# Node stage of a graph layer in pieces inside the edge loop, instead of a stage of its own behind it

## The chip, the cores and the metric

The kernel runs on one core of a Trainium2 chip. Its engines are TensorE (PE; PEld is its weight load), VectorE (DVE), ScalarE (ACT), GpSimd (POOL, "Pool" in the text) and SyncE (SP, which only issues DMAs here). Each engine works through its own list of instructions in order and waits on semaphores of the others. The metric is the device time of one execution in microseconds (us): 4080.77 before the change, the median of three runs (4079.7 to 4087.65).

## What is computed

A graph layer with attention over incoming edges, then a residual and a layer norm. There are 12,500 nodes with 64 features and 400,000 edges with 64 features, sorted by destination; the destinations are denser at low node numbers (12500 u² for uniform u).

```python
h_src = x[src]; h_dst = x[dst]
e = leaky_relu(concat([h_src, h_dst, edge]) @ W_attn + b_attn, 0.01)
m = concat([h_src, edge]) @ W_ne
ex = exp(e - segment_max(e, dst)[dst])
alpha = ex / segment_sum(ex, dst)[dst]
z = segment_sum(alpha[:, None] * m, dst)
out = relu(concat([x, z]) @ W_out)
return layernorm(x + out)
```

The kernel uses that W_ne is linear: it adds up alpha times (edge features, source features), 128 numbers for each node, and multiplies the sums by W_ne and the lower half of W_out at the end, as one 128x64 matrix named both.

## The kernel before

The sorted path (sorted_path, from line 40) makes a table of x with one more column, the source's part of the score, in DRAM, and windows of the destinations' parts. Then it goes over the edges. A group is 512 edges, four for each of the 128 partitions; there are 782 groups. A part is up to four groups (SG), and a batch is up to 24 groups, in six parts: batches 0 to 31 have 24 groups, batch 32 has 10 and batch 33 has 4 (the list sizes).

For each part, gather (line 137) loads the edge features ze by one DMA on SP's queue (L143), and the rows of the sources zx by 16 indirect DMAs on Pool (L152), one for each group and each of its four edges per partition. ze and zx have ten buffers each (ZB). scores (line 158) computes the scores of the part on DVE (L167 to L186) with one matmul on PE that spreads the windows (L163); its row wrow comes by a DMA on SP. hot marks each edge's place among the 48 nodes from its group's first destination on.

For each batch, softmax (line 226) runs segmented scans over the batch's scores. It is a serial chain of DVE, PE and ACT, from the transpose er at L254, over Exp on ACT (L298, L288), to alpha (L309, L310). Then aggregate (line 322) makes weights w from hot and alpha on DVE (L325), multiplies them with ze and zx on PE (L333, into one of four PSUM buffers named pg) and adds the result of each group on DVE to 48 columns of acc (L343). acc lies in SBUF and has a row for each of the 128 summed features and a column for each node.

The indices of batch k+2 are prepared in batch k: prepare, with a cast srcs on DVE (L121) into one of three buffers.

The node stage is in two places. In batches from 2 on, behind each part's aggregate, own_part (line 433) takes four node blocks of 128 nodes: it loads x (xb, L442, on ACT's queue), transposes it on PE (L447), copies it on ACT (L448), multiplies it with the upper half of W_out (L451), copies it (L453) and stores it in DRAM under the name early (L454). Behind the loop, finish_sorted (line 492) computes the flag that selects the general path, and both (L515 to L521), and then goes over the 98 blocks, eight at a time: it loads x again (L530) and early (L533), multiplies acc with both (L539), adds, takes relu and the residual, and normalizes (L548 to L562: eight steps on DVE, the square and the Sqrt on ACT), and stores the result (L565, L569).

The order of instructions on each engine is set when the program is built, by a scheduler that moves them by its own estimates; what a helper writes in one place can lie among the instructions of another on the engine. general_path is a second way to compute everything, which runs only where the flag is set.

Of the kernel before, what the change touches and what calls it, by code (L numbers as in the profile page):

```python
# [21 lines left out]
EPS = 1e-5  # L22
# [3 lines left out]
S = 48  # L26
BG = 32
SG = 4
# [3 lines left out]
ZB = 10  # L32
HB = 8
NBC = 4

BF16 = mybir.dt.bfloat16
EngineType = mybir.EngineType
# [2 lines left out]
def sorted_path(ctx, tc, x, dst, idx, edge, w_ne, w_attn, b_attn, w_out, out, flag):  # L40
# [38 lines left out]
    acc = const.tile([P, N + S], F32, name="acc")  # L79

    table = dram.tile([NB * P, EW], F32, name="table")
    early = dram.tile([NB * P, D], F32, name="early")
    sdflat = dram.tile([NB * P + S], F32, name="sdflat")
    shifted = dram.tile([NB * P, S], F32, name="shifted")
    wins = dram.tile([NG, S], F32, name="wins")
    d0i = const.tile([1, NG], I32, name="d0i")
    d0b = const.tile([P, NG], F32, name="d0b")
    worst = const.tile([P, 2], F32, name="worst")

    loop = ExitStack()  # L90
    chunks = loop.enter_context(tc.tile_pool(name="chunks", bufs=2))
# [254 lines left out]
    sizes = []  # L346
# [83 lines left out]
    nc.vector.memset(worst, 0.0)  # L430
    nc.vector.memset(acc, 0.0)

    def own_part(c0):

        n = min(NBC, NB - c0)
        xb = work.tile([P, NBC, D], F32, name="xb", bufs=1)
        if c0 + n > NFULL:
            nc.vector.memset(xb[:, n - 1, :], 0.0)
            nc.scalar.dma_start(out=xb[0:TAIL, n - 1, :], in_=x[NFULL * P:N, :])
        nf = min(n, NFULL - c0)  # L440
# [12 lines left out]
        nc.scalar.activation(xo[:, 0:n, :], po[:, 0:n, :], AF.Copy)  # L453
        nc.scalar.dma_start(out=early[c0 * P:(c0 + n) * P, :].rearrange("(b p) f -> p b f", p=P),  # L454
                            in_=xo[:, 0:n, :])

    def prepare(k):
        srcs, pp = prepared.pop(k) if k in prepared else indices(starts[k], sizes[k])
# [1 line left out]

    with loop:
        carry = None
        own = 0
        ready = {k: prepare(k) for k in range(2)}
        for k, G in enumerate(sizes):
            b0 = starts[k]
# [25 lines left out]
def finish_sorted(tc, x, out, acc, early, wne, wout, ident, worst, flag):  # L492

    nc = tc.nc
    N, D = x.shape
    NB = (N + P - 1) // P
    NFULL = N // P
    TAIL = N - NFULL * P
    NBF = 8
    with tc.tile_pool(name="fin", bufs=3) as fin, \  # L500
            tc.tile_pool(name="finp", bufs=2, space=bass.MemoryType.PSUM) as finp:

        bad = fin.tile([P, 2], F32, name="bad", bufs=1)
        nc.vector.tensor_scalar(bad[:, 0:1], worst[:, 0:1], float(S - 1), None, op0=OP.is_gt)
        nc.vector.tensor_scalar(bad[:, 1:2], worst[:, 1:2], 0.0, None, op0=OP.is_gt)
        pbad = finp.tile([1, 2, P], F32, name="pbad", bufs=1)
        for k in range(2):
            nc.tensor.matmul(pbad[:, k, :], bad[:, k:k + 1], ident, start=True, stop=True)
        some = fin.tile([1, 1], F32, name="some", bufs=1)
        nc.vector.tensor_reduce(some, pbad, axis=AX.XY, op=OP.max)  # L510
        nc.vector.tensor_copy(flag, some)


        pwt = finp.tile([D, P], F32, name="pwt", bufs=1)
        nc.tensor.transpose(pwt, wne, ident)  # L515
        wt = fin.tile([D, P], F32, name="wt", bufs=1)
        nc.vector.tensor_copy(wt, pwt)
        pv = finp.tile([P, D], F32, name="pwt", bufs=1)
        nc.tensor.matmul(pv, wt, wout[:, 1, :], start=True, stop=True)
        both = fin.tile([P, D], F32, name="both", bufs=1)  # L520
        nc.vector.tensor_copy(both, pv)  # L521
        for c0 in range(0, NB, NBF):
            n = min(NBF, NB - c0)
            xb = fin.tile([P, NBF, D], F32, name="xb")
            nf = min(n, NFULL - c0)
            if n > nf:
                nc.vector.memset(xb[:, n - 1, :], 0.0)
                nc.scalar.dma_start(out=xb[0:TAIL, n - 1, :], in_=x[NFULL * P:N, :])
            if nf:
                nc.scalar.dma_start(out=xb[:, 0:nf, :],  # L530
                                    in_=x[c0 * P:(c0 + nf) * P, :].rearrange("(b p) f -> p b f", p=P))
            xo = fin.tile([P, NBF, D], F32, name="xo")
            nc.sync.dma_start(out=xo[:, 0:n, :],  # L533
                              in_=early[c0 * P:(c0 + n) * P, :].rearrange("(b p) f -> p b f", p=P))
            po = finp.tile([P, NBF, D], F32, name="po")
            for j in range(n):
                k0 = (c0 + j) * P
                m = min(P, N + S - k0)
                nc.tensor.matmul(po[0:m, j, :], acc[:, k0:k0 + m], both, start=True, stop=True)  # L539
            yv = fin.tile([P, NBF, D], F32, name="yv")  # L540
            m = min(P, N + S - (c0 + n - 1) * P)
            if m < P:
                nc.vector.memset(yv[:, n - 1, :], 0.0)
                nc.vector.tensor_tensor(yv[0:m, n - 1, :], po[0:m, n - 1, :], xo[0:m, n - 1, :], op=OP.add)
                if n > 1:
                    nc.vector.tensor_tensor(yv[:, :n - 1, :], po[:, :n - 1, :], xo[:, :n - 1, :], op=OP.add)
            else:
                nc.vector.tensor_tensor(yv[:, :n, :], po[:, :n, :], xo[:, :n, :], op=OP.add)  # L548
            nc.vector.scalar_tensor_tensor(yv[:, :n, :], yv[:, :n, :], 0.0, xb[:, :n, :],
                                           op0=OP.max, op1=OP.add)  # L550
            stat = fin.tile([P, 2, NBF], F32, name="stat")
            nc.vector.tensor_reduce(stat[:, 0, :n], yv[:, :n, :], axis=AX.X, op=OP.add)
            nc.vector.tensor_scalar(stat[:, 0, :n], stat[:, 0, :n], 1.0 / D, None, op0=OP.mult)
            nc.vector.tensor_tensor(yv[:, :n, :], yv[:, :n, :],
                                    stat[:, 0, :n].unsqueeze(2).to_broadcast([P, n, D]), op=OP.subtract)
            sq = fin.tile([P, NBF, D], F32, name="sq")
            nc.scalar.activation(sq[:, :n, :], yv[:, :n, :], AF.Square)
            nc.vector.tensor_reduce(stat[:, 1, :n], sq[:, :n, :], axis=AX.X, op=OP.add)
            nc.vector.tensor_scalar(stat[:, 1, :n], stat[:, 1, :n], 1.0 / D, EPS, op0=OP.mult, op1=OP.add)
            nc.scalar.activation(stat[:, 1, :n], stat[:, 1, :n], AF.Sqrt)  # L560
            nc.vector.reciprocal(stat[:, 1, :n], stat[:, 1, :n])
            nc.vector.tensor_tensor(yv[:, :n, :], yv[:, :n, :],  # L562
                                    stat[:, 1, :n].unsqueeze(2).to_broadcast([P, n, D]), op=OP.mult)
            if nf:
                nc.sync.dma_start(  # L565
                    out=out[c0 * P:(c0 + nf) * P, :].rearrange("(b p) f -> p b f", p=P),
                    in_=yv[:, 0:nf, :])
            if n > nf:
                nc.sync.dma_start(out=out[NFULL * P:N, :], in_=yv[0:TAIL, n - 1, :])  # L569


def general_path(ctx, tc, x, dst, idx, edge, w_ne, w_attn, b_attn, w_out, out):
# [434 lines left out]
```

## Time and profile before

| | |
|---|---|
| median of three runs | 4080.77 us |
| the profiled execution | 4080.57 us |
| its span, first to last instruction | 4078.8 us |
| mean granted TensorE clock | 0.588 |
| busy: POOL, DVE, PE, PEld, ACT | 2967.8, 1875.2, 985.2, 766.8, 131.6 us |
| last row gather issued by Pool | 3970.51 us from the start |
| last add to acc | 4007.26 us, three adds, 0.68 us |
| first matmul of the stage behind the loop | 4010.83 us |
| last store issued | 4071.27 us |

A line of a timeline has the start in us, the duration in us, the engine, the line of the kernel, the operation, what it writes and reads with shapes, the count of instructions merged in the line, and in brackets how long the engine was idle before and what ended that. In a line of a group, the busy time and the mean ns of one stand behind the first bar, and the idle time before them behind the second. In a line of waits stand the total, the number and the longest. An engine named with a q (SPq, ACTq) is the queue that issues DMAs.

### The profile page before, as it was taken

What the parts mean: (1) busy time and instruction counts of PE and PEld (TensorE: products, weight loads), DVE (VectorE), ACT (ScalarE), POOL (GpSimd) and SP (SyncE); (2) the same over time, 40 slices, a digit from 0 to 9 for tenths busy, and PEclk for the clock granted to TensorE, in tenths of its full rate; (3) what the DMA queues carried; (4) which work ended last, traced back from release to release, by engine and by line L of the source; (5) the groups of instructions that cost most, each with busy time, mean ns of one, the idle gap of its engine ahead of it and who ended that gap; (6) DMA issues with size and microseconds to landing.
All of it is one profiled execution on the core that took longest, in us unless ns stands there. A gap on an engine that the chain in (4) does not pass through costs nothing.

```text
span 4078.8 us, 40728 instructions
## 1 busy us (share of the span) xinstructions
PE 985.2 (24%) x14494; PEld 766.8 (19%) x14494; DVE 1875.2 (46%) x4448; ACT 131.6 (3%) x287; POOL 2967.8 (73%) x3142
## 2 busy tenths in 40 slices
PE   0022332132222112222212222211222221122235
PEld 0022322122212011111101111211111120111225
DVE  4174443343555443455444355544335544434656
ACT  0000000000000000000000000000000000000001
POOL 6757777777777777777777777777777777777770
PEclk9985665565555555555555555555555555555555
DMA  8122332232222122222212222212222221222214
GB/s 169 29 51 60 75 75 57 46 74 60 60 60 60 28 59 59 59 60 60 48 39 59 59 60 59 60 34 54 59 60 60 60 59 27 59 58 58 55 26 96
DMA packets 315275, 239.80 MB, mean 59 GB/s; under 512 B 160574, under 2 KB 264233, under 8 KB 315062
## 3 DMA queue, kind: packets, MB, share of 16 engines
q0 software_dynamic: 100320, 104.42, 15.6%
q1 hardware_dynamic: 147462, 116.22, 9.6%
q10 hardware_dynamic: 67280, 16.45, 2.0%
q8 instruction: 117, 1.92, 0.2%
q14 instruction: 96, 0.79, 0.1%
HBM read 226.99 MB, written 12.28 MB: 59 GB/s over the span
## 4 chain that ended last, share of the span: by engine, by line
POOL 41%; DVE 22%; issue 17%; PE 11%; DMA 7%; ACT 1%; DVEq 0%; POOLq 0%; ACTq 0%
POOL zx L152 41%; DMA zx<-table,srcs 7%; PE pg L333 5%; DVE prod L167 3%; DVE y L169 3%; DVE prod L181 3%; PE fixed L163 2%; DVE hot L176 2%; PE sm L200 2%; PE sm L192 2%; DVE acc L343 1%; DVE sdst L184 1%; DVE by_row L197 1%; DVE b L273 1%; DVE w L325 1%
## 5 line engine op out<-in xcount | busy, mean ns | idle before, releaser
L152 POOL DMA_INDIRECT zx<-table,srcs x3032 | 2866.8, 946 | 956.7 <-issue 869.6
L163 PE MATMUL fixed<-wrow,ones_row 1*128 1x192 f32 x392 | 179.0, 553 | 2391.3 <-DVE prod L181 2314.5
L121 DVE CAST srcs<-pp 128x96 int32<-128x96 f32 (+2 forms) x34 | 8.6, 253 | 1587.0 <-DMA zx<-table,srcs 1521.5
L163 PEld LDWEIGHTS fixed<-wrow,ones_row 1*128 1x128 f32 x392 | 88.8, 280 | 2464.9 <-DVE prod L181 2385.1
L333 PE MATMUL pg<-w,ze 128*64 128x48 f32 x6256 | 459.3, 244 | 84.3 <-DVE w L325 73.4
L333 PEld LDWEIGHTS pg<-w,ze 128*64 128x64 f32 x6256 | 449.7, 161 | 104.5 <-DVE w L325 90.1
L333 PE MATMUL pg<-w,zx 128*64 128x48 f32 x6256 | 459.5, 244 | 5.3 <-issue 5.0
L333 PEld LDWEIGHTS pg<-w,zx 128*64 128x64 f32 x6256 | 449.7, 161 | 6.0 <-issue 6.0
L167 DVE TENSOR_TENSOR prod<-ze,fixed 128x1024 f32<-128x1024 f32 x196 | 237.6, 1212 | 86.4 <-DMA wins<-wk 49.9
L169 DVE TENSOR_REDUCE y<-prod 128x16 f32<-128x1024 f32 x196 | 237.2, 1210 | 0.0
L343 DVE TENSOR_TENSOR acc<-acc,pg 128x48 f32 x782 | 158.6, 203 | 164.1 <-PE pg L333 112.9
L325 DVE TENSOR_TENSOR w<-hot,fixed 128x768 f32<-128x768 bf16 x196 | 176.8, 944 | 42.9 <-PE pg L333 37.7
L184 DVE TENSOR_REDUCE sdst<-prod 128x16 f32<-128x768 f32 x196 | 186.1, 950 | 5.1
L181 DVE TENSOR_TENSOR prod<-hot,fixed 128x768 f32<-128x768 bf16 x196 | 185.5, 947 | 0.9
L176 DVE TENSOR_TENSOR hot<-fixed,drel 128x768 bf16<-128x768 f32 x196 | 185.9, 948 | 0.0
L115 ACT ACTIVATE nat<-raw 24x1024 f32<-24x1024 int32 (+2 forms) x34 | 35.9, 1056 | 2876.9 <-PE pp L118 2848.2
L152 POOL DMA_INDIRECT zx<-in_x_dram,srcs x96 | 93.5, 974 | 44.2 <-issue 28.7
L200 PE MATMUL sm<-ones_row,by_row 1*128 1x1 f32 x272 | 79.0, 357 | 108.9 <-DVE by_row L197 75.2
L200 PEld LDWEIGHTS sm<-ones_row,by_row 1*128 1x128 f32 x272 | 67.5, 307 | 176.8 <-DVE by_row L197 138.0
L192 PE MATMUL sm<-order,s 128*1 128x128 f32 x136 | 39.8, 396 | 194.6 <-DVE s L258 112.0
L118 PE MATMUL pp<-ident,nat 24*128 24x24 f32 (+2 forms) x272 | 36.3, 279 | 144.2 <-DVE drel L127 111.4
L174 DVE TENSOR_TENSOR y<-y,zx 128x16 f32<-128x16 f32 x196 | 37.0, 189 | 67.5 <-DMA zx<-table,srcs 64.4
(133 smaller groups left out, 1109.2 us busy)
## 6 DMA issues: line engine op xcount, KB each, us to landing
ze<-in_edge_dram SPq DMA_DIRECT2D x194, 512.0 KB
zx<-table,srcs POOLq DMA_INDIRECT x3032
table<-xt ACTq DMA_DIRECT2D x14, 227.5 KB
wrow<-wins SPq DMA_DIRECT2D x195, 0.8 KB
raw<-in_idx_dram SPq DMA_DIRECT2D x32, 96.0 KB
xb<-in_x_dram ACTq DMA_DIRECT2D x24, 128.0 KB
early<-xo ACTq DMA_DIRECT2D x24, 128.0 KB
xb<-in_x_dram ACTq DMA_DIRECT2D x12, 256.0 KB
```

Source lines behind the costliest of these rows:

```text
L152: nc.gpsimd.indirect_dma_start(out=zx[:, g, t, 0:D] if plain else zx[:, g, t, :], out_offset=None, in_=x[:, :] if plain else table[:, :], ...
L163: nc.tensor.matmul(win[:, 0:n, :], ones_row, wrow[:, 0:n, :], start=True, stop=True)
L167: nc.vector.tensor_tensor(prod[:, 0:n], ze[:, 0:n], w_edge.unsqueeze(1).to_broadcast([P, n, T, D]), op=OP.mult)
L169: nc.vector.tensor_reduce(yb, prod[:, 0:n], axis=AX.X, op=OP.add)
L176: nc.vector.tensor_tensor(hot[:, 0:n], slots.unsqueeze(1).unsqueeze(1).to_broadcast([P, n, T, S]), drel[:, :, b:b + n].rearrange("p t g -> ...
L181: nc.vector.tensor_tensor(at[:, 0:n], hot[:, 0:n], win[:, 0:n].unsqueeze(2).to_broadcast([P, n, T, S]), op=OP.mult)
L184: nc.vector.tensor_reduce(sdst[:, 0:n], at[:, 0:n], axis=AX.X, op=OP.add)
L192: nc.tensor.matmul(p[0:1, :], col, order, start=True, stop=True)
L200: nc.tensor.matmul(p[:, 0:1], by_row, ones_row[:, 0:1], start=True, stop=True)
L325: nc.vector.tensor_tensor(w[:, 0:n], hot[:, 0:n], alpha[:, :, b:b + n].rearrange("p t g -> p g t").unsqueeze(3).to_broadcast([P, n, T, S]) ...
L333: nc.tensor.matmul(pg[at:at + D, g, :], z[:, g, t, 0:D], w[:, g, t, :], start=(t == 0), stop=(t == T - 1))
L343: nc.vector.tensor_tensor(ag, ag, pg[:, g, :], op=OP.add)
```

## The change

The stage behind the loop and the early product go. In their place a function finish takes four node blocks through the whole node stage: the load of x, the transposes, both products, added up in one PSUM tile, and then relu, residual and norm, in that tile, and the store from SP's queue. A plan made when the program is built (due) says after which batch each piece can be done. It takes the square root of the share of nodes as the share of edges, with eight standard deviations (LATE) and a quarter of a group on top, and finds the first batch that starts beyond that. A piece is issued behind a part of scores in the batch that follows.

The boundaries are checked on the chip: after each batch with due pieces, one DVE operation takes the first destination of the next batch less the end of the pieces, and keeps the minimum in a column early; where it is negative, the flag is set and the general path runs. Before, early was the DRAM buffer; that buffer, its stores and loads are gone.

For this input's 34 batches the plan has 25 pieces. Pieces that start at blocks 0 to 80 (21 of them) run in batches 7 to 31, some batches with none and two with two; pieces 84 and 88 run in batch 32, 92 in batch 33, and the last, with blocks 96 and 97, behind the loop.

```diff
+LATE = 8.0
-    early = dram.tile([NB * P, D], F32, name="early")
+    early = const.tile([P, 1], F32, name="early")
+    both = const.tile([P, D], F32, name="both")
...
+    pwt = psum.tile([P, SG, P], F32, name="pg", bufs=4)
+    nc.tensor.transpose(pwt[0:D, 0, :], wne, ident)
+    wt = work.tile([D, NBC, P], F32, name="xtt", bufs=1)
+    nc.vector.tensor_copy(wt[:, 0, :], pwt[0:D, 0, :])
+    nc.tensor.matmul(pwt[:, 1, 0:D], wt[:, 0, :], wout[:, 1, :], start=True, stop=True)
+    nc.vector.tensor_copy(both, pwt[:, 1, 0:D])
...
-    def own_part(c0):
+    def finish(c0):
         n = min(NBC, NB - c0)
         xb = work.tile([P, NBC, D], F32, name="xb", bufs=1)
...
         for j in range(n):
             nc.tensor.transpose(pxt[0:D, j, :], xb[:, j, :], ident)
         nc.scalar.activation(xtt[:, 0:n, :], pxt[0:D, 0:n, :], AF.Copy)
-        po = psum.tile([P, NBC, P], F32, name="pg", bufs=4)[:, :, 0:D]
+        po = psum.tile([P, NBC, P], F32, name="pg", bufs=4)[:, 0:n, 0:D]
         for j in range(n):
-            nc.tensor.matmul(po[:, j, :], xtt[:, j, :], wout[:, 0, :], start=True, stop=True)
-        xo = work.tile([P, NBC, D], F32, name="xo", bufs=1)
-        nc.scalar.activation(xo[:, 0:n, :], po[:, 0:n, :], AF.Copy)
-        nc.scalar.dma_start(out=early[...], in_=xo[:, 0:n, :])
+            nc.tensor.matmul(po[:, j, :], xtt[:, j, :], wout[:, 0, :], start=True, stop=False)
+            nc.tensor.matmul(po[:, j, :], acc[:, (c0 + j) * P:(c0 + j + 1) * P], both, start=False, stop=True)
+        nc.vector.scalar_tensor_tensor(po, po, 0.0, xb[:, 0:n, :], op0=OP.max, op1=OP.add)
+        mean = tiny.tile([P, NBC], F32, name="mean")[:, 0:n]
+        nc.vector.tensor_reduce(mean, po, axis=AX.X, op=OP.add)
+        nc.vector.tensor_scalar(mean, mean, 1.0 / D, None, op0=OP.mult)
+        nc.vector.tensor_tensor(po, po, mean.unsqueeze(2).to_broadcast([P, n, D]), op=OP.subtract)
+        sq = work.tile([P, NBC, D], F32, name="sq", bufs=1)
+        nc.scalar.activation(sq[:, 0:n, :], po, AF.Square)
+        var = tiny.tile([P, NBC], F32, name="var")[:, 0:n]
+        nc.vector.tensor_reduce(var, sq[:, 0:n, :], axis=AX.X, op=OP.add)
+        nc.vector.tensor_scalar(var, var, 1.0 / D, EPS, op0=OP.mult, op1=OP.add)
+        nc.scalar.activation(var, var, AF.Sqrt)
+        nc.vector.reciprocal(var, var)
+        yo = work.tile([P, NBC, D], F32, name="yo", bufs=1)
+        nc.vector.tensor_tensor(yo[:, 0:n, :], po, var.unsqueeze(2).to_broadcast([P, n, D]), op=OP.mult)
+        nc.sync.dma_start(out=out[...], in_=yo[...])
...
+    due = [[] for _ in sizes]
+    k = 0
+    for c0 in range(0, NB, NBC):
+        share = min(1.0, (c0 + NBC) * P / N) ** 0.5
+        need = E * share + LATE * (E * share * (1.0 - share)) ** 0.5 + GE / 4
+        while k + 1 < len(sizes) and starts[k + 1] * GE < need:
+            k += 1
+        due[k].append(c0)
...
                 parts.append((g0, n, ze, zx, hot))
+                if done:
+                    finish(done.pop(0))
...
                 aggregate(g0, n, ze, zx, hot, b0, fac if g0 == b0 else None)
-                if own < NB and k > 1:
-                    own_part(own)
-                    own += NBC
-        while own < NB:
-            own_part(own)
-            own += NBC
-    finish_sorted(tc, x, out, acc, early, wne, wout, ident, worst, flag)
+            done += due[k]
+            if due[k] and k + 1 < len(sizes):
+                nc.vector.scalar_tensor_tensor(early, d0b[:, starts[k + 1]:starts[k + 1] + 1],
+                                               -float((due[k][-1] + NBC) * P), early, op0=OP.add, op1=OP.min)
+        bad = tiny.tile([P, 3], F32, name="bad")
...
+        nc.vector.tensor_scalar(bad[:, 2:3], early, 0.0, None, op0=OP.is_lt)
...
+        nc.vector.tensor_reduce(some, pbad, axis=AX.XY, op=OP.max)
+        nc.vector.tensor_copy(flag, some)
+        for c0 in done:
+            finish(c0)
```

More of the change, by code (lines that the diff above doesn't have):

```diff
@@ L431, in sorted_path @@
     nc.vector.memset(acc, 0.0)
-    def own_part(c0):
+    pwt = psum.tile([P, SG, P], F32, name="pg", bufs=4)
[5 more added lines that the diff above has]
+    def finish(c0):
         n = min(NBC, NB - c0)
         xb = work.tile([P, NBC, D], F32, name="xb", bufs=1)
-        if c0 + n > NFULL:
+        nf = min(n, NFULL - c0)
+        if n > nf:
             nc.vector.memset(xb[:, n - 1, :], 0.0)
             nc.scalar.dma_start(out=xb[0:TAIL, n - 1, :], in_=x[NFULL * P:N, :])
-        nf = min(n, NFULL - c0)
         if nf:
@@ L448, in own_part @@
         nc.scalar.activation(xtt[:, 0:n, :], pxt[0:D, 0:n, :], AF.Copy)
-        po = psum.tile([P, NBC, P], F32, name="pg", bufs=4)[:, :, 0:D]
+        po = psum.tile([P, NBC, P], F32, name="pg", bufs=4)[:, 0:n, 0:D]
         for j in range(n):
-            nc.tensor.matmul(po[:, j, :], xtt[:, j, :], wout[:, 0, :], start=True, stop=True)
-        xo = work.tile([P, NBC, D], F32, name="xo", bufs=1)
-        nc.scalar.activation(xo[:, 0:n, :], po[:, 0:n, :], AF.Copy)
-        nc.scalar.dma_start(out=early[c0 * P:(c0 + n) * P, :].rearrange("(b p) f -> p b f", p=P),
-                            in_=xo[:, 0:n, :])
+            nc.tensor.matmul(po[:, j, :], xtt[:, j, :], wout[:, 0, :], start=True, stop=False)
+            nc.tensor.matmul(po[:, j, :], acc[:, (c0 + j) * P:(c0 + j + 1) * P], both, start=False, stop=True)
@@ new lines, in finish @@
+        var = tiny.tile([P, NBC], F32, name="var")[:, 0:n]
[5 more added lines that the diff above has]
+        nc.vector.tensor_tensor(yo[:, 0:n, :], po, var.unsqueeze(2).to_broadcast([P, n, D]), op=OP.mult)
+        if nf:
+            nc.sync.dma_start(out=out[c0 * P:(c0 + nf) * P, :].rearrange("(b p) f -> p b f", p=P),
+                              in_=yo[:, 0:nf, :])
@@ L457, in prepare @@
+        if n > nf:
+            nc.sync.dma_start(out=out[NFULL * P:N, :], in_=yo[0:TAIL, n - 1, :])
+    due = [[] for _ in sizes]
[6 more added lines that the diff above has]
+        due[k].append(c0)
+    nc.vector.memset(early, 0.0)
     def prepare(k):
@@ L462, in sorted_path @@
         carry = None
-        own = 0
+        done = []
         ready = {k: prepare(k) for k in range(2)}
@@ L482, in sorted_path @@
                 aggregate(g0, n, ze, zx, hot, b0, fac if g0 == b0 else None)
-                if own < NB and k > 1:
-                    own_part(own)
-                    own += NBC
-        while own < NB:
-            own_part(own)
-            own += NBC
-    finish_sorted(tc, x, out, acc, early, wne, wout, ident, worst, flag)
[L492 to L503, printed above, removed]
+            done += due[k]
@@ L504, in finish_sorted @@
+            if due[k] and k + 1 < len(sizes):
+                nc.vector.scalar_tensor_tensor(early, d0b[:, starts[k + 1]:starts[k + 1] + 1],
+                                               -float((due[k][-1] + NBC) * P), early, op0=OP.add, op1=OP.min)
+        bad = tiny.tile([P, 3], F32, name="bad")
         nc.vector.tensor_scalar(bad[:, 0:1], worst[:, 0:1], float(S - 1), None, op0=OP.is_gt)
         nc.vector.tensor_scalar(bad[:, 1:2], worst[:, 1:2], 0.0, None, op0=OP.is_gt)
-        pbad = finp.tile([1, 2, P], F32, name="pbad", bufs=1)
@@ L507, in finish_sorted @@
-        for k in range(2):
+        nc.vector.tensor_scalar(bad[:, 2:3], early, 0.0, None, op0=OP.is_lt)
+        pbad = psum.tile([P, 3, P], F32, name="sm")[0:1]
+        for k in range(3):
             nc.tensor.matmul(pbad[:, k, :], bad[:, k:k + 1], ident, start=True, stop=True)
-        some = fin.tile([1, 1], F32, name="some", bufs=1)
+        some = tiny.tile([1, 1], F32, name="some")
         nc.vector.tensor_reduce(some, pbad, axis=AX.XY, op=OP.max)
         nc.vector.tensor_copy(flag, some)
-        pwt = finp.tile([D, P], F32, name="pwt", bufs=1)
@@ L515, in finish_sorted @@
[L515 to L569, printed above, removed]
```

## Prediction

> **What bounds the kernel now.** I read the page's busy times and chain first, then Pool's waits, then the DVE, ACT and SP timelines of the last 170 us.
>
> ```profile
> POOL 41%; DVE 22%; issue 17%; PE 11%; DMA 7%; ACT 1%; DVEq 0%; POOLq 0%; ACTq 0%
> ```
> ```profile
> L152 POOL DMA_INDIRECT zx<-table,srcs x3032 | 2866.8, 946 | 956.7 <-issue 869.6
> ```
> ```profile
> POOL zx L152 <- issue: 898.3, 2947, 0.3
> POOL zx L152 <- DMA zx<-table,srcs: 33.2, 109, 0.3
> POOL zx L152 <- PE pg L333: 33.2, 2, 32.9
> ```
>
> In the chain Pool's row gathers and the gap ahead of each make up most. A gather takes 0.95 us, the gap is 0.30, so one starts every 1.25 us; that pitch holds from 260 us to the last gather. Pool waits once for another engine (32.9 us, until batch 0 is aggregated at 260) and never again. So until its last gather nothing else counts, unless it makes Pool wait. The last gather and what follows:
>
> ```profile
> 3970.51 0.94 POOL L152 DMA_INDIRECT zx<-table,srcs  x1 [0.30 <-issue]
> ```
> ```profile
> 3783.20 0.17 DVE L121 CAST srcs<-pp 128x16 int32<-128x16 f32 x1 [53.92 <-DMA zx<-table,srcs]
> ...
> 3953.07 0.17 DVE L174 TENSOR_TENSOR y<-y,zx 128x8 f32<-128x8 f32 x1 [2.40 <-DMA zx<-table,srcs]
> ...
> 3985.70 0.31 DVE L254 STREAM_TRANSPOSE er<-y 128x128 f32<-128x128 f32 x1
> ...
> 4007.26 0.68 DVE L343 TENSOR_TENSOR acc<-acc,pg 128x48 f32 x3
> ...
> 4014.54 0.69 DVE L548 TENSOR_TENSOR yv<-po,xo 128x512 f32<-128x512 f32 x1 [3.77 <-PE po L539]
> ...
> 4070.55 0.29 DVE L562 TENSOR_TENSOR yv<-yv,stat 128x128 f32<-128x128 f32 x1
> ```
>
> DVE idles some 53 us in each full batch (first line), so there is room for it there. From 3953.07 it is nearly always busy or waiting a fraction of a microsecond on PE: softmax and aggregation of the ten-group batch 32, scores (end 3985.7), softmax and aggregation (end 4007.94) of the four-group batch 33, then 70.9 us of node stage to the span's end at 4078.8. The profiled execution took 4080.57 us, 1.77 outside the span; the median of the runs is 4080.77, 0.2 more.
>
> **Removed: the node stage at the end.** From 4007.94 to 4078.8: 70.86 us. The early partial product in batches 2 to 7 (25 pieces, its store and the later reload) goes too, worth nothing: it lies beside gathers that never waited for it.
>
> **Added at the end.** Only the last piece (two blocks) is behind the last add. PE's last aggregation matmul ends about 4006.85; two transposes 0.7, ACT's copy 0.38 (row for 64x256) and hand-offs to 4008.1; then four matmuls at 0.42 (the L539 row, at a granted clock of 0.5) and 0.35 until DVE sees it: 4010.15, that is 2.2 after the last add. Then, by the two-block rows at 4065.99 to 4070.84: 0.29 + 0.28 + 0.12 + 0.28 with gaps 1.17; square 0.40; the switch to the Sqrt table; Sqrt 0.20, reciprocal 0.17, product 0.29, gaps 0.1.
>
> The switch: in the old stage the square ends at 4023.32, the table load stands at 4024.29 for 1.28 us and Sqrt starts at 4025.58, 2.26 in all. The Trainium skill (ScalarE: Activation LUTs, section What ACT_TABLE_LOAD costs) puts a switch at 1.28 load plus 1.38 drain, 2.66. The row says 0.4 less, and I take the row: 4.6 for the chain (5.0 by the rule). The rule speaks against the change, too: one switch becomes 43 (to Sqrt and back to Exp in 21 batches, and one at the end), 114 us if they lay on the path. They don't: beside gathers ACT is idle, and in both short batches ACT stands 5.2 to 5.3 us between the copy of the scores and the first Exp, in which 2.26 fits. In batch 33 two switches share that gap plus the piece's delay; about 0.4 us is left.
>
> After the last DVE instruction the old kernel needed 7.96 us (4070.84 to 4078.8: two stores of a single block, and the end); I keep that. New end: 2.2 + 4.6 + 7.96 = 14.8 instead of 70.86, **−56.1 us**.
>
> **Added in the short batches.** By the scheduled order, pieces 84 and 88 lie among batch 32's scores and piece 92 among batch 33's, all in DVE's stream and ahead of a softmax. A piece issues on DVE five operations over 128x256 and three over 128x4. The 128x512 rows take 0.69, so 0.36; small ones 0.17, partly overlapped; 2.05 a piece. That a result goes back to PSUM no row shows: I take the row with a PSUM source (L548), bounds 0 and +0.36 for two of them in each piece.
>
> - Piece 84 needs the last add of batch 31 (3940.24), then seven matmuls at 0.42 and 0.35: 3943.55. DVE is free at 3941.2 and waits 2.3.
> - Piece 88 reads xb, which has one buffer, so its load is issued when 84's first DVE operation is done (3943.9). The one landing of this load on the chain took 3.89 us (bounds 2.6, as other 128 KB transfers, and 5): 3947.85; transposes 1.1, copy 0.6, eight matmuls 3.4, 0.35: 3953.4. DVE gets there at 3950.6 and waits 2.8. Behind it on DVE are the scores of parts 2 and 3, behind its matmuls on PE the window row of part 3.
> - The 2.40 wait for gathers at 3953.07 goes. Sum: 2.3 + 2.8 + 2 x 2.05 − 2.4 = **+6.8** (0 to 12).
> - Piece 92: adds of batch 32 end at 3981.25, matmuls 3.3 later; DVE waits 1.3. Its first four operations overlap to 1.0; the others sit in PE waits of 0.68, 0.2 left. The flag's reduction, before at 4009.14 and 0.41 us over 256, is now over 384 and stands ahead of alpha: 0.5. **+3.0** (1 to 6).
>
> **Added in the other batches.** 21 pieces run in batches 7 to 31. SP's stores wait for DVE with window rows behind them, PE's matmuls wait for acc with the next window row behind. The cover is DVE's 53 us per batch. Pool feels it only through the buffers: part 5 of batch 31 starts gathering at 3861.8 (3970.51 less 87 gathers at 1.25) into a buffer that PE freed about 3829: 32 us to spare, against two pieces and waits of some 10. Nothing; if that cover were gone, a piece would cost its 2.05 us of DVE and 3 to 5 of waits, 21 times 5 to 7. The 23 small operations of 0.15 that keep the check of the boundaries lie under the same cover.
>
> **At the start** the product of weights lies in DVE's stream ahead of batch 0's softmax, on the path to Pool's only stall: a copy of 0.23 and one small operation, **+0.4**.
>
> Sum: 4078.8 − 56.1 + 6.8 + 3.0 + 0.4 = 4032.9; plus 1.77 = 4034.7 for an execution like the profiled one, 4034.9 against the median. I say **4035**.
>
> **Rivals.**
> 1. *DVE locks Pool out, and it gets slower.* The Trainium skill (SBUF — State Buffer, section Who interferes with whom) says that copies and tensor_scalar on VectorE can take a port pair that GpSimd needs to write descriptors, and hold it for the whole instruction; it measures a 0.62 us transfer at 3.1, 2.5 more. 23 pieces now run beside gathers, each with eight DVE operations. The mechanism decides from 2.0 us per piece on (23 x 2.0 = 46 takes the whole gain); with two operations of each piece holding a gather by 2.5 it is 23 x 5 = 115 and 4150 us, slower than before. Against it: beside today's gathers run copies, casts and tensor_scalars in every softmax, and the pitch over 200 us windows is 1.249 to 1.252, the longest single one 1.43. The new big operations have a PSUM operand, which the page excludes, and the small ones are 128x4. By the row: nothing. 5%, 3 of them slower than before and 2 a hold that just eats the gain.
> 2. *The short batches cost more*: results in PSUM slow, the xb load late under gathers, Exp waiting for its table. +12 for batch 32, +6 for 33, 5 at the end: 4044 to 4055. 10%.
> 3. *They cost nothing*, because waits overlap where I added them: 4035 − 9.8 = 4025. 5%.
> 4. *The flag trips* and the general path runs: at least another 3128 gathers at 1.25, 3,900 us more. From the plan's formula and the sorted destinations, the first destination after each boundary lies 70 to 619 nodes beyond the pieces finished there, so no. Under 1%.
>
> **Numbers.** The forecast has 79%: 4035, with 4027 to 4044. The range 4026 to 4050 reaches over half of rival 2 and leaves out some 15%. A measurement of this kernel tells about 0.2% (8 us) from no change. Faster 94%: the forecast, rivals 2 and 3; slower 4%: the larger part of rival 1, and rival 4; within 0.2% 2%: the rest of rival 1.
>
> **What would show it.** Pool's last gather near 3971 and its pitch 1.25: if later, rival 1 or a buffer. The transpose of batch 32's scores (3954.7 before) at 3961.5, that of batch 33 near 3995, the last add near 4018, the last DVE product near 4025, 8 us before the end. ACT's table loads should be short and waited for by nobody but the last Sqrt. The forecast is wrong if Pool waits for PE or DVE after 260, or if the last add comes after 4025.

## The result, and the profile after

The changed kernel takes 4029.55 us (median of four runs, 4028.22 to 4036.38) against 4080.23 (four runs of the kernel before, 4079.2 to 4087.65): a ratio of 0.9876, 95% interval 0.986 to 0.9891, some 51 us less. The forecast was 4035, with 4026 to 4050. The profiled execution was the longest of the four, 4036.38 us with a span of 4034.7; a later one of the same kernel, the run named again below, has a span of 4027.2, and both are used.

The chain that ended last, the row gathers and Pool's waits, of the profiled execution after (columns as in the prediction; the lines of the code are two further down):

```profile
POOL 41%; DVE 23%; issue 17%; PE 10%; DMA 7%; ACT 1%; DVEq 0%; POOLq 0%; ACTq 0%
```
```profile
L154 POOL DMA_INDIRECT zx<-table,srcs x3032 | 2870.8, 947 | 957.1 <-issue 880.3
```
```profile
POOL zx L154 <- issue: 908.9, 2981, 0.3
POOL zx L154 <- PE pg L335: 33.6, 3, 32.9
POOL zx L154 <- DMA zx<-table,srcs: 25.6, 84, 0.3
```

The shares are those of before to within a point. There is still the one stall of 32.9 us, and behind it no wait above the gap of 0.3: none of the new work holds a gather. The general path did not run, since the gathers are still 3,032. The last gather and what follows it, on the timeline of the same execution:

```profile
3976.99 0.95 POOL L154 DMA_INDIRECT zx<-table,srcs  x1 [0.30 <-issue]
```
```profile
3949.53 0.43 DVE L462 SCALAR_TENSOR_TENSOR pg<-pg,xb 128x256 f32<-128x256 f32 x1 [2.49 <-PE pg L461]
...
3959.44 0.43 DVE L462 SCALAR_TENSOR_TENSOR pg<-pg,xb 128x256 f32<-128x256 f32 x1 [3.17 <-PE pg L461]
...
3967.17 0.31 DVE L256 STREAM_TRANSPOSE er<-y 128x128 f32<-128x128 f32 x1
...
3999.49 0.31 DVE L256 STREAM_TRANSPOSE er<-y 128x128 f32<-128x128 f32 x1
...
4021.00 0.92 DVE L345 TENSOR_TENSOR acc<-acc,pg 128x48 f32 x4 [3.78 <-PE pg L335]
4024.60 0.30 DVE L462 SCALAR_TENSOR_TENSOR pg<-pg,xb 128x128 f32<-128x128 f32 x1 [2.68 <-PE pg L461]
...
4027.70 0.17 DVE L473 RECIPROCAL var<-var 128x2 f32<-128x2 f32 x1 [1.02 <-ACT var L472]
4027.91 0.29 DVE L475 TENSOR_TENSOR yo<-pg,var 128x128 f32<-128x128 f32 x1
```

L462 is the first operation of a piece on DVE: pieces 84 and 88 wait 2.49 and 3.17 for PE, then come the scores of batch 32 (er at 3967.17), those of batch 33 (3999.49), the last adds (end 4021.92), and two blocks of node stage to 4028.20. The span ends 6.5 us later. All these times lie 6.5 us later than they would by the last gather of before (3970.51), so I read them from that gather on: from its start to the end of the span were 108.29 us before and are 57.71 now. The forecast had 62.0.

### The profile page after: what moved, and what is told of

Same layout as the page of the kernel before. It is cut to its first block, busy times and chain, and to the rows that moved or that the text cites. A ratio compares the mean times of both kernels' runs of the same rounds, so it can differ in the third digit from the quotient of the medians.

```text
span 4034.7 us, 40868 instructions
## 1 busy us (share of the span) xinstructions
PE 1025.7 (25%) x14496; PEld 786.8 (20%) x14496; DVE 1866.9 (46%) x4553; ACT 180.4 (4%) x328; POOL 2972.8 (74%) x3142
## 4 chain that ended last, share of the span: by engine, by line
POOL 41%; DVE 23%; issue 17%; PE 10%; DMA 7%; ACT 1%; DVEq 0%; POOLq 0%; ACTq 0%
POOL zx L154 41%; DMA zx<-table,srcs 6%; PE pg L335 4%; DVE prod L169 3%; DVE y L171 3%; DVE prod L183 3%; DVE hot L178 2%; PE fixed L165 2%; PE sm L194 2%; PE sm L202 2%; DVE sdst L186 1%; DVE by_row L199 1%; DVE b L275 1%; DVE w L327 1%; DVE acc L345 1%
```

## The experiments

Two measures are used for each run: the median of its times, and from its trace the start of the last gather and the time from there to the end of the span, called the tail. The tail takes out what the gathers themselves vary by. The pitch is the mean time from the start of one gather to that of the next, behind the one stall.

| run | median us (range) | ratio to before (interval) | last gather | tail | mean pitch after the stall |
|---|---|---|---|---|---|
| before (profiled) | 4080.23 | | 3970.51 | 108.29 | 1.2504 |
| changed (profiled) | 4029.55 (4028.22 to 4036.38) | 0.9876 (0.986 to 0.9891) | 3976.99 | 57.71 | 1.2518 |
| again | 4029.06 (4028.66 to 4029.78) | 0.9871 (0.9855 to 0.9888) | 3969.36 | 57.84 | 1.2496 |
| every_part | 4036.19 (4035.22 to 4040.1) | 0.9892 (0.9876 to 0.9909) | 3969.32 | 64.48 | 1.2500 |
| twice | 4031.15 (4030.98 to 4032.19) | 0.9877 (0.9861 to 0.9893) | 3970.98 | 59.22 | 1.2500 |
| with_early | 4028.75 (4028.32 to 4031.67) | 0.9873 (0.9857 to 0.989) | 3969.08 | 57.82 | 1.2498 |
| all_behind | 4253.2 (one run) | | 3971.84 | 279.46 | 1.2504 |
| no_tail_pieces | 4020.73 (4019.6 to 4021.52) | 0.9851 (0.9835 to 0.9868) | 3967.79 | 50.01 | 1.2496 |
| xb2 | 4028.83 (4027.32 to 4030.56) | 0.9872 (0.9855 to 0.9888) | 3968.34 | 57.26 | 1.2497 |
| warm_sqrt | 4029.11 (4028.38 to 4030.78) | 0.9873 (0.9856 to 0.9889) | 3969.04 | 57.66 | 1.2497 |
| late4 | 4030.04 (4029.3 to 4030.24) | 0.9858 (0.9842 to 0.9875) | 3975.61 | 52.89 | 1.2516 |
| best | 4028.58 (4027.61 to 4032.7) | 0.9858 (0.9841 to 0.9874) | 3974.56 | 52.24 | 1.2515 |
| again2 | 4029.12 (4028.4 to 4029.94) | 0.9874 (0.9858 to 0.989) | 3969.02 | 57.88 | 1.2497 |
| best2 | 4022.69 (4021.88 to 4024.84) | 0.9859 (0.9843 to 0.9875) | 3968.28 | 52.62 | 1.2495 |

late4 and best ran on another chip than the other experiments, where the kernel of before took 4088.07 us (4086.0 to 4089.35) instead of 4081.3 to 4081.8; they are compared with the rest by ratio and tail only.

**Again: the changed kernel as it is.** Its question is whether the 6.5 us by which the last gather moved belong to the change.

> The changed kernel once more, nothing edited. In its first profiled execution Pool's last gather began at 3976.99 us, 6.5 later than before the change. Theory (the pieces cost Pool nothing; the 6.5 us belong to that execution): a median of 4028 to 4031, and in a second profile a last gather at 3969 to 3974, with 57 to 58 us from it to the span's end, as in the first. Rival (the pieces beside the gathers slow Pool): the last gather near 3977 again, with a pitch of 1.251 to 1.252 where pieces run.

The last gather is at 3969.36, 1.15 us earlier than before and 7.6 earlier than in the profiled execution, while the tail is the same, 57.84 against 57.71. So the 6.5 us are no effect of the change. Of the 7.6 us between these two executions of one kernel, 6.3 are the pitch, 1.2518 against 1.2496 over 2,967 gathers, and 1.3 are a later restart behind the stall (262.98 against 261.65). The kernel before does the same: the longest of its runs, 4087.65 us, stands some 7 to 8 us above the other three.

**Every part: is a piece beside gathers free?** A finished piece is done again behind every part of scores that has no new one, in batches up to 31. 154 pieces run instead of 25.

```diff
+        seen = []
...
                 if done:
-                    finish(done.pop(0))
+                    seen.append(done.pop(0))
+                    finish(seen[-1])
+                elif seen and k < 32:
+                    finish(seen[-1])
```

> A piece behind each of the six parts of batches 7 to 31: the piece that is due, and in the parts without one the latest again; some 150 instead of 21. At 2.05 us of DVE and 3 to 6 us of waits for PE a piece, six take 30 to 50 us of a batch's 53 us of idle time. Theory: still no change of the last gather to within 5 us, since a batch just holds them; if the waits are longer, the cover is gone and Pool falls behind by up to 10 us a batch, 250 us in all. Rival (port): 129 more pieces at 2 to 5 us, 260 to 650 us more, with a pitch clearly above 1.25.

The last gather is at 3969.32, where it was, with 129 pieces more. DVE's own waits show where they went. From 262 to 3935 us, the longest of them: ahead of again, then of this run.

```profile
DVE srcs L123 <- DMA zx<-table,srcs: 1442.7, 30, 66.3
```
```profile
DVE srcs L123 <- DMA zx<-table,srcs: 985.8, 30, 66.0
DVE pg L462 <- PE pg L461: 362.6, 126, 4.3
```

The cover, DVE's wait in each batch until gathers have landed, fell by 457 us, 3.5 for each additional piece, and 986 us of it are left. The time did rise, by 7.1 us, 6.6 of it in the tail, which the expectation did not have. DVE's last wait of that kind ahead of batch 32, in again, and then the last two repeats in this run:

```profile
3901.90 0.19 DVE L176 TENSOR_TENSOR y<-y,zx 128x16 f32<-128x16 f32 x1 [14.58 <-DMA zx<-table,srcs]
```
```profile
3898.86 0.43 DVE L462 SCALAR_TENSOR_TENSOR pg<-pg,xb 128x256 f32<-128x256 f32 x1 [2.61 <-PE pg L461]
...
3908.84 0.43 DVE L462 SCALAR_TENSOR_TENSOR pg<-pg,xb 128x256 f32<-128x256 f32 x1 [2.68 <-PE pg L461]
```

The last repeat lies behind that wait, where nothing covers it, and the first L462 of batch 32 comes at 3948.56 instead of 3942.00, with the last gather unmoved. So a piece beside gathers is free up to the last wait for gathers in batch 31.

**Twice: the same at a smaller dose.** Each piece up to batch 31 is done two times, 46 in all.

```diff
-                    finish(done.pop(0))
+                    c0 = done.pop(0)
+                    finish(c0)
+                    if k < 32:
+                        finish(c0)
```

> Every piece that runs in batches 7 to 31 is done twice, 21 pieces more beside gathers, the same results stored twice. Theory (DVE idles some 53 us per batch and Pool has 32 us to spare in the buffers): no change of the time within 0.2%, the last gather where it was, pitch 1.250 to 1.252. Rival (operations on DVE hold Pool off its port): 2 to 5 us per piece, 40 to 100 us more.

It is 2.1 us slower than again by the medians. The tail is 1.4 longer: the transpose er of batch 32 lies 8.2 us ahead of the last gather instead of 9.8. The repeat in batch 31 is not what does it: both its pieces run ahead of the last two waits for gathers, and the softmax of batch 31 stands where it did (its L302 is 55.9 us ahead of the last gather, 55.8 in again). The difference comes behind it, on PE: over the matmuls of piece 84 the granted clock is 0.50 here and 0.72 in again, and L462 waits 3.50 us for them instead of 2.47. Whether that is so in all four runs can't be told from one trace. The last gather of this one trace is 1.6 later; of that nothing can be said, since the changed kernel's own last gather is at 3969.02, 3969.36 and 3976.99 in three executions, and since every_part, with a larger dose, has it at 3969.32.

**With early: the removed product, put back.** The early product of before runs again as dead work behind each part's aggregate, with its loads and with its stores into a buffer that nobody reads.

```diff
                 aggregate(g0, n, ze, zx, hot, b0, fac if g0 == b0 else None)
+                if own < NB and k > 1:
+                    own_part(own)
+                    own += NBC
...
```

> The early product of batches 2 to 7, which the change removed, is put back beside the pieces: its loads, transposes, matmuls, copies and stores run, and nothing reads what they store. Theory (it lay under the gathers): no change within 0.2%. Rival (part of what was won is its removal): up to 10 us more, with the last gather later by as much.

4028.75 us, and a tail of 57.82: no difference. What was removed from batches 2 to 7 was worth nothing, as its place beside gathers says.

**All behind: the same pieces in the old place.** The pieces stay as they are, but all 25 run behind the loop.

```diff
-                if done:
-                    finish(done.pop(0))
```

> The plan is kept, but no piece runs inside the loop: all 25 stand behind it, in the form of the changed kernel (both products in one PSUM tile, four blocks, one buffer each). Theory (a piece is a serial chain when nothing covers it: load 3.9 if not fetched ahead, transposes and copy 2, matmuls 3.7, DVE and ACT some 4.5): 10 to 14 us a piece, 240 to 340 us more than the changed kernel, near 4300, far slower than before the change. Rival (the gain comes from the fused form, not from the place): near 4080 or less.

4253.2 us in one run, which is 224 more than the changed kernel and 172 more than the kernel before. DVE's first operations of the first three pieces:

```profile
4014.01 0.43 DVE L462 SCALAR_TENSOR_TENSOR pg<-pg,xb 128x256 f32<-128x256 f32 x1 [3.92 <-PE pg L461]
...
4023.50 0.43 DVE L462 SCALAR_TENSOR_TENSOR pg<-pg,xb 128x256 f32<-128x256 f32 x1 [5.26 <-PE pg L461]
...
4033.04 0.43 DVE L462 SCALAR_TENSOR_TENSOR pg<-pg,xb 128x256 f32<-128x256 f32 x1 [5.91 <-PE pg L461]
```

A piece of four blocks takes 9.5 us when nothing hides it, a little under the 10 to 14 expected. The old stage took 70.86 us for 98 blocks, 2.9 for four, with the product by the upper half of W_out already done. So the new form is over three times as dear for a block; the gain is the place alone.

**No tail pieces: what the three pieces in the short batches cost.** Pieces 84, 88 and 92 are left out, so 1,536 nodes get no result.

```diff
-                    finish(done.pop(0))
+                    c0 = done.pop(0)
+                    if c0 < 84:
+                        finish(c0)
```

> Leaves out the pieces that start at blocks 84, 88 and 92 (1,536 nodes get no result). It measures the price of the three pieces in the short batches. By the traces they cost 5.95 and 1.4 us ahead of the two softmaxes and 0.2 behind: 7.0 to 8.0 us less, 49.7 to 50.7 from the last gather to the end. By the forecast 9.8 less the flag's 0.5, 9.3. Rival (the pieces' time lies beside waits that stay without them): under 4.

8.3 us less by the medians, and 7.83 in the tail. By steps, against again: up to the transpose er of batch 32 5.99 less, so that it lies 15.80 ahead of the last gather as before the change (15.77); to that of batch 33 1.59 less; from there to the last add the same within 0.1; from the last add to the last product 1.31 less; and from there to the end 1.01 more. The third was no part of any theory. Granted clock (the column behind ACT's and POOL's busy times) over the two-block piece's matmuls and what ran just ahead; this run first, then again:

```profile
4002.50:4004.10 1.60, 1.60 (x34) 1.55 (x30) 0.00 (x0) 0.00 (x0) 0.00 (x0) 0.52 0.02 5
4004.90:4006.60 1.70, 1.52 (x8) 1.18 (x8) 0.30 (x3) 0.05 (x1) 0.00 (x0) 1.00 0.02 5
```
```profile
4014.39:4016.95 2.56, 2.53 (x8) 1.99 (x8) 0.00 (x0) 0.00 (x0) 0.00 (x0) 0.50 0.02 6
```

The same four matmuls (two instructions each) ran at a granted clock of 1.00 in 1.5 us, and at 0.50 in 2.5. That is no part of the pieces' price, which is then 5.99 + 1.59 = 7.6 us.

**A second buffer for xb.** In my sum, the wait of piece 88 was there because its load could start only when piece 84 had released xb.

```diff
-        xb = work.tile([P, NBC, D], F32, name="xb", bufs=1)
+        xb = work.tile([P, NBC, D], F32, name="xb", bufs=2)
```

> Two buffers for xb, so that the load of the second piece of batch 32 needn't wait until the first piece has read its own. Theory (the wait of 3.17 us in front of the second piece's first DVE operation is this load and what hangs on it): 2 to 3.2 us less from the last gather to the end, 54.5 to 55.7. Rival (the eight matmuls on PE and the order of the engines set that wait, not the load): less than 1 us.

Nothing by the medians (4028.83 against 4029.06), 0.4 us in the place of er: the rival holds. The load was indeed taken out of the path. DVE's first operation of piece 88 and what stands around it in DVE's stream, in this run:

```profile
3943.46 0.16 DVE L465 TENSOR_SCALAR mean<-mean 128x4 f32<-128x4 f32 x1
3946.25 0.43 DVE L462 SCALAR_TENSOR_TENSOR pg<-pg,xb 128x256 f32<-128x256 f32 x1 [2.63 <-issue]
3946.59 0.17 DVE L187 TENSOR_TENSOR sdst<-sdst,y 128x16 f32<-128x16 f32 x1
```

and PE's last matmul pairs of that piece and the window row behind them:

```profile
3944.85 0.69 PE L460 MATMUL pg<-wout,xtt 64*128 64x64 f32 x2
3945.47 0.69 PE L461 MATMUL pg<-both,acc 128*128 128x64 f32 x2
3946.09 1.00 PE L165 MATMUL fixed<-wrow,ones_row 1*128 1x192 f32 x2
```

Counted from the last gather, L462 is 4.5 us earlier than in again (3951.82 there), and still DVE stood idle for 2.63 us ahead of it, with the last steps of part 1's scores (L187) and all of part 2's waiting in line behind. The view gives no releaser, but the time is PE's: its last matmul of the piece starts at 3945.47, and L462 follows when it is through. PE went almost without a break from piece 84 to piece 88, and its eight matmuls for the piece at 0.62 each, 4.9 us, are more than the 2.1 us that DVE works in between. The load was one of two waits that ended close together; taking away one showed the other.

**Sqrt's table loaded ahead.** A Sqrt of one column ahead of the last piece, while ACT is idle.

```diff
+        warm = tiny.tile([P, 1], F32, name="warm")
+        nc.scalar.activation(warm, fac, AF.Sqrt)
         for c0 in done:
             finish(c0)
```

> One Sqrt on a spare column ahead of the last piece, after the last Exp, so that the Sqrt table is loaded under the last aggregation. From the row (the reciprocal of the last piece waited 1.02 us for Sqrt, with a load of 1.28 straight behind the square): 0.7 to 1.0 us shorter from the last gather to the end, 56.7 to 57.0 instead of 57.7. If a switch costs 2.66 us wherever it lies, as the page has it, 2 us or more.

Nothing by the medians, and 0.2 in the tail instead of the 0.7 to 1.0 expected. ACT's timeline of the last piece, again and then this run:

```profile
4018.24 0.28 ACT L468 ACTIVATE sq<-pg 128x128 f32<-128x128 f32 x1 [3.90 <-DVE pg L466]
4018.53 1.28 ACT L472 ACT_TABLE_LOAD   x1
4019.83 0.20 ACT L472 ACTIVATE var<-var 128x2 f32<-128x2 f32 x1
```
```profile
4017.94 0.28 ACT L468 ACTIVATE sq<-pg 128x128 f32<-128x128 f32 x1 [3.90 <-DVE pg L466]
4018.77 0.20 ACT L472 ACTIVATE var<-var 128x2 f32<-128x2 f32 x1 [0.56 <-DVE var L471]
```

The table load is gone from there, and from the end of the square to Sqrt it is 0.55 us instead of 1.31: the load had hidden the reduction of sq and the scaling of var, which are next late. From the last add to the last product it is 5.51 instead of 6.25. Of these 0.74 us the end kept 0.2, since the issue of the last store took longer. SP's last two lines, again and this run:

```profile
4020.59 0.35 SPq L477 DMA_DIRECT2D out_dram<-yo  x1
4020.99 0.41 SPq L480 DMA_DIRECT2D out_dram<-yo  x1
```
```profile
4019.53 0.35 SPq L477 DMA_DIRECT2D out_dram<-yo  x1
4019.93 0.99 SPq L480 DMA_DIRECT2D out_dram<-yo  x1
```

That issue took 0.41 to 0.48 us in ten traces of the changed kernel and its variants, and 0.79, 0.99 and 1.67 in best2, here and in no_tail_pieces. Why is not settled.

**Half the margin, and a faster version.** no_tail_pieces says that 6.0 of 7.6 us belong to batch 32, which has two pieces. With four standard deviations instead of eight, the plan puts piece 84 into batch 31, among gathers; pieces 36, 40 and 44 come one batch earlier too, among gathers before and after. late4 has this alone; best adds the second buffer (of xtt too) and the early Sqrt.

```diff
-LATE = 8.0
+LATE = 4.0
```

> The margin LATE is halved from 8 to 4 standard deviations, so that piece 84 becomes due one batch earlier, in batch 31, among gathers; batch 32 keeps piece 88 alone. My theory (what a piece costs in a short batch is PE's eight matmul pairs, 4.9 us, and the 2.05 us of DVE; beside gathers it costs nothing): the wait of 3.2 us for the second piece and its 2.05 us of DVE leave batch 32, the wait of some 2.5 us for the first stays, and some of the wait for gathers may return: 3 to 5 us faster than the changed kernel, 4024 to 4026 us, with the last gather where it was. Rival (the pieces' place does not matter, the short batch is set by gathers or by softmax): within 1 us of 4029.

> The halved margin as in the run beside it, a second buffer for xb and for xtt, and a Sqrt on a small tile ahead of the last piece, so that the table is loaded before. My theory: the margin gives its 3 to 5 us; the second buffers give little more now that batch 32 has one piece (0 to 0.5 us); the early table load takes 1.0 us off the chain behind the last add: 4022.5 to 4025.5 us. Rival (the end is set by the last store and not by the chain ahead of it): the early load gives nothing again, and the time is that of the run beside it.

late4's tail is 52.89, 4.95 less than again's, and er of batch 32 lies 14.9 ahead of the last gather (9.8 in again): the move of one piece gives back five of the six microseconds. The piece that stays costs some 0.9 (er lies 15.8 ahead without any):

```profile
3948.23 0.43 DVE L462 SCALAR_TENSOR_TENSOR pg<-pg,xb 128x256 f32<-128x256 f32 x1 [1.93 <-PE pg L461]
...
3960.72 0.31 DVE L256 STREAM_TRANSPOSE er<-y 128x128 f32<-128x128 f32 x1
```

Its wait of 1.93 us (2.47 in again, where the granted clock over its matmuls was 0.72 instead of 0.90 here) and its some 2 us of work stand mostly in the place of the wait for gathers that batch 32 had before, 2.40 us. The ratio of late4 is 0.9858 against 0.9871. The medians of late4 and best missed their ranges (4024 to 4026, 4022.5 to 4025.5), but the chip's gathers were slower, 1.2516 and 1.2515, so that the time in microseconds shows nothing by itself. best's tail is another 0.65 less. To see the gain in the time, best ran once more, under the name best2, on one chip with the changed kernel (again2):

> The changed kernel as it is, on the same chip as the version beside it. In the two runs before this one a chip whose gathers start every 1.2515 us instead of 1.2495 put the last gather 6 us later and moved the kernel of before with it. So its ratio to the kernel of before is to be 0.9871 again, within 0.001, and from the last gather to the span's end 57.7 to 57.9 us, whatever the chip's pitch is.

> The halved margin, the second buffers and the early Sqrt, beside the changed kernel on one chip. My theory: from the last gather to the span's end 52.2 us against 57.8, so 5 to 6 us faster than the run beside it (0.14%). Rival (what the trace shows is given back elsewhere, in later gathers): within 2 us of it.

4022.69 (4021.88 to 4024.84) against 4029.12 (4028.4 to 4029.94): 6.4 us faster, with ranges apart; 5.3 of it in the tail, 0.7 in the start of the last gather. This is the fastest kernel with the whole result here, 59 us below the kernel before. The smaller margin makes it likelier that some input crosses a boundary and pays for the general path; on this input none is crossed.

## Why the prediction was right, and where it missed

The theory holds: the node stage was on the path only because it lay behind the last gather, beside gathers it is free (up to the last wait for them in batch 31), and what remains is the short batches and the end. Its rivals fall: the lock by every_part, the dearer short batches by a tail of 57.8 instead of the 71 to 82 that 4044 to 4055 us means, the flag by the number of gathers, and the free short batches by no_tail_pieces, which puts them at 7.6 us. The size was off by 5.7 us in the span, of which 1.55 lie in the gathers, as follows (measured: again, worked out from its trace against the trace of before).

| term | forecast | measured |
|---|---|---|
| last gather | +0.4 | −1.15 |
| batch 32, two pieces | +6.8 | +5.96 |
| batch 33 up to its transpose er | +2.3 | +1.36 |
| batch 33 behind it (flag) | +0.7 | +0.19 |
| last add to the last piece's first DVE operation | 2.2 | 2.66 |
| from there to the last product | 4.6 | 3.59 |
| last product to the end | 7.96 | 6.65 |
| span | 4032.9 | 4027.2 |

- **Gathers.** The lock between DVE and Pool was weighed at 2.0 us a piece as the point of decision. 129 additional pieces moved the pitch from 1.2496 to 1.2500, 1.1 us in all, 0.01 for each piece. The rule of the Trainium skill (SBUF — State Buffer, Who interferes with whom) leaves out a VectorE operation with at most one SBUF input outside the two-port modes, and says that a reduction has no such mode; of the five large operations of a piece four have a PSUM operand, which leaves them one SBUF input at most, and the fifth, L470, which the prediction passed over, is a reduction. The run agrees with that, and says nothing on long copies within SBUF. The +0.4 at the start can't be told: the restart behind the stall is at 262.98, 261.65 and 261.04 in three runs of one kernel, 260.67 before.
- **Batch 32.** The waits, 2.47 and 3.09 in again, are near the 2.3 and 2.8 of the sum, but the second by two errors that cancel, which is luck. Piece 88 in again, its load, transposes, first and last matmuls and first DVE operation:

```profile
3942.46 0.37 ACTq L451 DMA_DIRECT2D xb<-in_x_dram  x1
3945.01 1.03 PE L456 MATMUL pg<-ident,xb 128*64 128x128 f32 x4 [0.67 <-DMA xb<-in_x_dram]
3946.79 0.68 PE L460 MATMUL pg<-wout,xtt 64*128 64x64 f32 x2 [0.74 <-ACT xtt L457]
...
3951.10 0.69 PE L461 MATMUL pg<-both,acc 128*128 128x64 f32 x2
3951.82 0.43 DVE L462 SCALAR_TENSOR_TENSOR pg<-pg,xb 128x256 f32<-128x256 f32 x1 [3.09 <-PE pg L461]
```

Its load took 2.5 us (from issue at 3942.46 to the transposes at 3945.01), not the 3.89 of the chain's row. Its eight matmuls took 5.0 (3946.79 to 3951.82), not 3.4: I took 0.42 us from the old stage's long run of matmuls, and in the pieces, where those over 64 and over 128 rows alternate, one takes 0.62 at the same granted clock of 0.50; why is not shown. The same 0.62 makes the wait behind the last add 2.66 instead of 2.2. So the cause I named for piece 88's wait, the single buffer of xb, did not set it alone: xb2 takes it away, and the wait falls only from 3.09 to 2.63. DVE's own work for both pieces is 3.95 us, counted from each start to the next on its timeline, as the 4.1 had it. What makes the sum smaller than its parts is the batch's own work: its scores, interleaved with the pieces, take 0.75 less than before, and they begin 0.5 earlier against the last gather.

- **Batch 33 and the flag** came out at 1.55 instead of 3.0: the piece waits 0.88 us for PE, not 1.3; its operations behind er cost nothing, since from er to the transpose of alpha it is 16.07 us with them and 16.14 in no_tail_pieces without; and of the flag's reduction (0.53 us for 1x384) about half lies in a wait that was there before (15.86 from er to alpha then). That DVE waits only a fraction of a microsecond on PE from 3953.07 on was not so: ahead of the last adds it waits 3.78.
- **The table switch.** I read 2.26 us between the square and Sqrt in the trace of before and took it for the switch. It is 1.31: the load of 1.28 stands directly behind the square, and Sqrt directly behind the load. The Trainium skill (ScalarE: Activation LUTs, What ACT_TABLE_LOAD costs) has 1.28 for the load, as here, and 1.38 more to drain, 2.66 in all; nothing here shows the second part. The line that I passed over stands in ACT's timeline of before, between the two that I read:

```profile
4022.69 0.63 ACT L557 ACTIVATE sq<-yv 128x512 f32<-128x512 f32 x1 [20.44 <-DMA xb<-in_x_dram]
4023.88 0.38 ACTq L530 DMA_DIRECT2D xb<-in_x_dram  x1
4024.29 1.28 ACT L560 ACT_TABLE_LOAD   x1 [0.97 <-DVE yv L549]
```

The table load stood in line behind a DMA issue on ACT's queue, which waited for DVE to release xb (L549, end 4023.85). The bracket of the load even names DVE, so the gap ahead of it was a wait. The other 42 switches (the profile after counts 22 loads at L472 and 21 at L300, 1,283 ns each) cost next to nothing, as forecast. From 262 to 3935 us, DVE's waits for Exp, before and then in again:

```profile
DVE s L289 <- ACT ex L288: 13.2, 31, 0.4
```
```profile
DVE s L291 <- ACT ex L290: 12.6, 31, 0.7
```

The longest is 0.3 us longer, the sum no larger.

- **The end.** From the last product to the end of the span it is 6.35 to 7.7 us in thirteen traces of the changed kernel and its variants, 7.96 before. Carrying the old figure over was 1.3 too much. SP's own waits at the branch that skips the general path are 2.4 to 2.8 us in the traces of the changed kernel and its variants and 4.1 before, which is about the difference; what ends them is open.

## What to carry to other kernels

When one engine's stream sets the pace, ask of every stage whether it can lie beside that stream before asking how fast it is: here a stage in a form three times as dear for a block, where nothing hides it, made the kernel 1.2% faster. Work is free only as long as its batch has cover, so the last, short batches deserve their own sum, and moving one of the two pieces out of batch 32 returned five of the six microseconds that they cost there. Before taking a gap from a trace as the price of an operation, read that engine's queue lines between its ends, and the releaser named in the bracket.

## What the runs showed of the hardware that was not expected

- The pitch of the indirect gathers differs by chip or execution, 1.2495 to 1.2518 us in kernels with the same gathers; over 2,967 of them that is 7 us, more than most edits here. Only runs beside each other on one chip, or times measured from the last gather, tell such edits apart.
- TensorE's granted clock over the last piece's four matmuls was 1.00 in no_tail_pieces and 0.50 in again and every other run of the changed kernel and its variants, 1.3 us apart on the path. In again and in no_tail_pieces, some 3.6 us of aggregation matmuls run just ahead. The Trainium skill (TensorE: Matmul & The Clock Gate, Part 1: The HAM clock gate) says that the clock rises after about 3.4 us of sustained work, counted in windows that run freely; a stretch of 3.6 us may then fall on either side. The clocks fit this: in all fourteen traces the granted clock is 0.5 or 1.0 and nothing between, and each stretch at 1.0 lasts a whole multiple of 3.41 us, 13.65 most often. No run here moves the work against the windows to test it.
